# Paired Softplus, a column projection in rows of eight and a later load of the residual in a four-image scan, attention and spectral-filter kernel

## Chip, core and metric

The kernel runs on one core of a Trainium2 chip. The metric is the device time of one execution in microseconds (us). Before the change it is 5593.63 us, the median of 3 runs (5587.63 to 5597.1).

TensorE (PE, with its weight loads shown as PEld), VectorE (DVE), ScalarE (ACT), GpSimd (POOL) and SyncE (SP, which here does nothing but issue DMAs) each run a list of instructions of their own in order. They wait for one another through semaphores.

## The reference

Four images of 48 x 48 tokens and 128 channels (2304 tokens an image) pass through a state-space layer, an attention and a causal spectral filter, each with a residual:

```python
# layer 0: four scan directions k over the image after in-projection, 3x3 conv, silu
x0 = xc.reshape(B, d, L)                                  # row order
x1 = jnp.transpose(xc, (0, 1, 3, 2)).reshape(B, d, L)     # column order
xs = jnp.stack([x0, x1, x0[..., ::-1], x1[..., ::-1]], axis=1)
x_dbl = jnp.einsum('bkdl,kcd->bkcl', xs, x_proj_w)        # the x-projection
dts_r, Bs, Cs = (x_dbl[:, :, :R], x_dbl[:, :, R:R + N], x_dbl[:, :, R + N:])
dts = jnp.einsum('bkrl,kdr->bkdl', dts_r, dt_proj_w)
dt = jax.nn.softplus(dts + dt_proj_b[None, :, :, None])
...
def step(h, inp):
    dt_l, u_l, B_l, C_l = inp
    dA = jnp.exp(dt_l[..., None] * A)
    h = h * dA + (dt_l * u_l)[..., None] * B_l[:, :, None, :]
    y = jnp.einsum('bkdn,bkn->bkd', h, C_l)
    return (h, y)
...
# layer 1
t = t + _L1_attn_ref(_ln_t(t))
t = t + _L1_ffn_ref(_ln_t(t), ...)    # 16 causal FFT filters, projected and summed ("STU")
```

There are d = 256 inner channels and N = 16 states, so a direction has 4096 scans of 2304 steps.

## The kernel before

**Stages.** For each image b: a prologue (norm, in-projection, conv, silu), then the scans of the four directions, then an epilogue and the attention. The spectral filter of image b - 1 is worked out on TensorE during the scans of image b (`stu`, line 1060), interleaved by a count of matmul columns. During the scans of image 0 its place is taken by a mixture of filter weights (line 901); the filter of the last image stands alone at the end (`stu3`, line 1355). The prologue of the next image and the first part of its scans' preparation lie between the steps of the attention.

**Scans.** A direction is cut into 6 chunks of 384 columns, so an image has 24 chunks (k = 0 to 3). A chunk has 8 units (two halves h of the channels, four groups q of states), and a unit has four scans of 128 rows x 384 columns (`TENSOR_TENSOR_SCAN`, line 511). That is 192 units and 768 scans an image. For a unit, ScalarE writes the four decays exp(dt A) (line 504) and a copy of the B row (line 487) into slots of a ring in PSUM. VectorE multiplies (line 495) and scans. Three of eight units have their product on GpSimd instead, and need no copy of B. GpSimd multiplies the scanned states by C (line 521), and TensorE sums them over states (line 529). The ring has five slots for image 0 and four for the others.

**Preparation of a chunk** (`Chunk.prep`, line 380) is a generator that is advanced three times a unit, from 17 units ahead of the chunk's first (`LEAD`) over 15 units (`STEPS`). It makes, in order: the x-projection into a ring slot (line 408) and its copy to `xd` on ScalarE (line 413), for k = 0 and 1 only; the store of it (line 429; k = 2 and 3 load it again, since they run over the same columns backwards); two dt projections (line 422), each copied from a ring slot (line 425); Softplus over 128 x 768 in place (line 434), between two table loads of ScalarE, since it and exp are in different tables; the product dt x (line 452); two stores (line 441); and loads of `rep`, four DMAs for each half (line 446), that spread rows over partitions. `fetch` (line 467) brings the B and C rows, 32 DMAs a chunk (line 473).

**Order.** Schedules are written by hand: each engine's instructions stand in the order in which the Python code issues them. All DMAs that matter here are on SyncE's queue. It issues them in order, and an issue that waits holds all those behind it. Before the scans of image b + 1, `begin_scans` (line 553) advances chunk 0's preparation to its end, fetches its 32 rows, and advances those of chunks 1 and 2 a little. It is a generator too, one step for each step of the attention. The attention ends with the division of its output into `T` (lines 1013 to 1020), its store (line 1022, `td`), a load of part of it (`tu`, line 1028), a norm and transposition into `uT` (line 1053), and the store of that (`ud`, line 1055), for five pieces J of the tokens. The scans' tiles `s` take the SBUF space that `T` held.

**The spectral filter** runs over blocks of tokens and, in each, over 16 filters k. `begin` (line 1180) loads a block's input (`ux`), weights (`mue`) and residual (`res`, from `td`). `ended` (line 1242) adds the projected result to the residual (line 1244) and stores the output.

Of the kernel before, what the change touches and what calls it, by code (L numbers as in the profile page):

```python
# [8 lines left out]
F32 = mybir.dt.float32  # L9
AF = mybir.ActivationFunctionType  # L10
ALU = mybir.AluOpType
# [4 lines left out]
P = 128  # L16
B, H, W, C = 4, 48, 48, 128
# [3 lines left out]
NH = D // P  # L21
CS = 384
# [3 lines left out]
KF = 16  # L26
# [33 lines left out]
def hybrid_kernel(ctx: ExitStack, tc: tile.TileContext, a: dict, out: bass.AP):  # L60
# [3 lines left out]
    nc = tc.nc  # L64
# [3 lines left out]
    res = ctx.enter_context(tc.tile_pool(name="res", bufs=1, space=DRAM))  # L68
# [16 lines left out]
    xw = load("xw", [P, NH, 2, P], a["x_proj_wT"].rearrange("(h p) k r -> p h k r", p=P))  # L85
# [35 lines left out]
    onerow = wp.tile([P, 1], F32, name="onerow")  # L121
# [48 lines left out]
    class Slow:  # L170


        def __init__(self, f, w):
            self.f, self.w = f, w
# [153 lines left out]
    def in_order(t, k, lo, n):  # L328

        if k % 2 == 0:  # L330
            return t[:, lo // W:(lo + n) // W, :]
        return t.rearrange("p h w -> p w h")[:, lo // H:(lo + n) // H, :]
# [33 lines left out]
    class Chunk:  # L366


        def __init__(self, b, k, c):
            self.b, self.k, self.lo = b, k, c * CS  # L370
            self.name = f"{b}_{k}_{c}"
            self.bc, self.rep = {}, []
            self.rev = k >= 2
            self.first = c == (NCH - 1 if self.rev else 0)
            self.last = c == (0 if self.rev else NCH - 1)

            self.slot = CS if self.rev else 0
            self.at = slice(0, CS) if self.rev else slice(1, CS + 1)

        def prep(self, pool):  # L380

            k, name, xc = self.k, self.name, xcs[self.b]
            xdd_ = xdd[k % 2][self.lo // CS]

            def rest(n=1):

                yield
                yield 0
                yield
                for i in range(3 * n - 3):
                    yield 0 if i % 3 == 1 else None

            if k >= 2:
                xd = self.xd = pool.xd.tile([P, CS], F32, tag="xd", name=f"xd{name}")
                nc.sync.dma_start(xd, xdd_)
            yield from rest(2)  # L400
            if k < 2:
                hold = mm_hold()
            yield
            if k < 2:
                xd = self.xd = pool.xd.tile([P, CS], F32, tag="xd", name=f"xd{name}")
                ps = mm_tile(f"xp{name}", hold)
                for h in range(NH):
                    nc.tensor.matmul(ps[:, :CS], xw[:, h, k, :], in_order(xc[h], k, self.lo, CS),
                                     start=(h == 0), stop=(h == NH - 1))
            yield 2 * CS if k < 2 else 0  # L410
            yield
            if k < 2:
                nc.scalar.activation(xd, ps[:, :CS], AF.Identity, bias=onerow)
                mm_done(hold)
            yield from rest()

            re = pool.one.tile([P, NH, 2, CS], F32, tag="re", name=f"re{name}")
            for h in range(NH):
                hold = mm_hold()
                yield  # L420
                ps = mm_tile(f"dt{name}_{h}", hold)
                nc.tensor.matmul(ps[:, :CS], dtw[:, k, h * P:(h + 1) * P], xd, start=True, stop=True)
                yield CS
                yield
                nc.scalar.copy(re[:, h, 0], ps[:, :CS])
                mm_done(hold)
                if h == 0:
                    if k < 2:
                        nc.sync.dma_start(xdd_, xd)
                    yield from rest()  # L430
            yield
            yield 0

            nc.scalar.activation(re[:, :, 0], re[:, :, 0], AF.Softplus)
            yield
            yield
            yield 0
            d = dram.tile([NH, G4, DL, 2, CS], F32, tag="dtdu", name=f"dtdud{name}")

            def store(h):  # L440
                nc.sync.dma_start(d[h].rearrange("g j i t -> (g j) i t"), re[:, h])

            def load(h):
                rep = pool.rep.tile([P, G4, 2, CS], F32, tag="rep", name=f"rep{name}_{h}")
                for c in range(C4):
                    nc.sync.dma_start(rep[c::C4], d[h].rearrange("g j i t -> j g i t"))
                self.rep.append(rep)

            for h in range(NH):
                x = in_order(xc[h], k, self.lo, CS)  # L450
                dt, dx = [re[:, h, i].rearrange("p (r w) -> p r w", w=x.shape[2]) for i in range(2)]
                nc.vector.tensor_tensor(dx, dt, x, ALU.mult)
            yield
            yield
            store(0)
            yield 0
            store(1)
            yield
            yield from rest(2)
            load(0)  # L460
            yield from rest(2)
            yield
            yield 0
            load(1)
            yield
# [78 lines left out]
    POOLED = ((0, 3), (1, 1), (1, 3))  # L544
    order = [(k, c) for k in range(K) for c in (range(NCH) if k < 2 else reversed(range(NCH)))]
    quads = [(h, q) for h in range(NH) for q in range(Q4)]
    STEPS = 15
    LEAD = 17
    FETCHED = range(2 * Q4)

    CHUNK_COLS = len(quads) * CS + 3 * CS

    def begin_scans(b, pool):

        chunks = [Chunk(b, k, c) for k, c in order]
        preps = [ch.prep(pool) for ch in chunks]
        for i in range(7):
            next(preps[0])
        for i in range(3 * STEPS - 7):
            if next(preps[0]) is not None:  # L560
                yield
        for i in FETCHED:
            chunks[0].fetch(i, pool)
        for i in range(3 * (LEAD - len(quads))):
            if next(preps[1]) is not None:
                yield
        for i in range(3 * (LEAD - 2 * len(quads))):
            next(preps[2])
        yield chunks, preps

    def scans(b, chunks, preps, front, sp, back, ring, finish, work, work_cols):
# [39 lines left out]
        def prepare(s):  # L611

            ci, j = divmod(s, len(quads))
            for c in range(ci + 1, ci + 4):
                if c < len(chunks) and 0 <= s - len(quads) * c + LEAD < STEPS:
                    done[0] += next(preps[c]) or 0

        def refill(s, i):
# [46 lines left out]
            next(finish, None)  # L665
        for u in pending:
            u.add_y()
        assert next(work, None) is None

# [388 lines left out]
    def stu(b, env, seeds):  # L1060
# [15 lines left out]
        items = [(blk, k) for blk in BLOCKS for k in range(KF)]  # L1076
        tts, Gs, U, now, nxt = {}, {}, {}, {}, [0]
# [21 lines left out]
        order = [(n, cs) for n in range(len(items)) for cs in slots(n)]  # L1099
# [80 lines left out]
        def begin(n):  # L1180
            (lo, hi, place, extra), k = items[n]
            m = 2 if extra else 1

            now["x"] = pool.one.tile([P, 6, P], F32, tag="ux", name=f"ux{b}_{n}")
            nc.sync.dma_start(now["x"][:, 2:, :hi - lo], ud[:, :, 1 + lo:1 + hi])
            nc.sync.dma_start(now["x"][:, :2, :hi - lo], ud[:, 2:, lo:hi])
            now["mu"] = pool.one.tile([P, 2, 3, C], F32, tag="mue", name=f"mue{b}_{n}")
            nc.sync.dma_start(now["mu"][:, :m], mud[:, place:place + m])
            now["T", n] = pool.two.tile([P, 4, C], F32, tag="res", name=f"res{b}_{n}")
            nc.sync.dma_start(now["T", n][:hi - lo], td[4 * lo:4 * hi].rearrange("(p j) c -> p j c", j=4))  # L1190

        def parts(w, extra):
# [57 lines left out]
        tabs, ps, pool = env  # L1250
        prime()
        for n, (_, k) in enumerate(items):
            if k == 0:
                begin(n)
            yield from conv(n, 0)
            if n > 0:
                fetch_G(n - 1)
            if n > 1:
                if k == 2:
                    yield from ar(n - 2)  # L1260
                yield from project(n - 2)
            for c in (2, 1):
                yield from conv(n, c)
            if n > 1 and k == 1:
                do_late()
                yield from end(n - 2)
        n = len(items) - 1
# [236 lines left out]
    SB = bass.MemoryType.SB  # L1504
# [38 lines left out]
    run(prologue(0, turn.one, mm_tile), 3, weights(once.one))  # L1543
    turn.close()
    once.close()
    front = Stage(tc, "f0", "left", one=(1, SB), xd=(3, SB), rep=(3, SB))
    first = begun(begin_scans(0, front))
    begin0.close()
    start_y(0)
    for b in range(B):  # L1550
        sp = Stage(tc, f"h{b}", "left", s=(6, SB))
        ps = Stage(tc, f"b{b}", "right", psa=(1, PSUM), psy=(1, PSUM), psc=(1, PSUM), psp=(1, PSUM))
# [34 lines left out]
        if more:  # L1587
            env = [tabs]
            work = stu_alone(b, env)
# [17 lines left out]
                parts.pop(0)()  # L1607
        if more:
            turn.close()
            front = Stage(tc, f"f{b + 1}", "left", one=(1, SB), xd=(3, SB), rep=(3, SB))  # L1610
            start_y(b + 1)
            pieces = begin_scans(b + 1, front)
        first = None
# [81 lines left out]
```

## Time and profile before

| | |
|---|---|
| median of 3 runs | 5593.63 us (5587.63 to 5597.1) |
| profiled execution, its own time | 5603.98 us |
| its span, first to last instruction | 5602.2 us |
| mean granted TensorE clock | 0.930 |
| scans of images 0, 1, 2, 3, first to last (us in the span) | 120 to 1072, 1320 to 2322, 2566 to 3566, 3807 to 4805 |
| busy share of the span | PE 86%, DVE 78%, POOL 65%, ACT 59%, PEld 55% |
| table loads before Softplus, before exp | 95 and 89, 1283 ns each |

The whole span, in 40 slices of 140 us, with the busy share of each engine in tenths:

```profile
PE   3566556698999998898999999898999999889999
DVE  6999999856899999756999999657999999513211
ACT  2777777546777776456777776457777776432111
POOL 1899999714889998505888998406889998301100
```

VectorE is full during the four stages of scans (slices 2 to 8, 10 to 17, 19 to 26, 28 to 35). Between them lie the ends of the attention, and after the last the spectral filter of image 3, on TensorE alone. In the tables that follow, a group's line gives its count, its busy time, the mean of one in ns, and the idle time of its engine just before it with what ended most of it. A timeline's line gives the start, the duration, the instructions, and in brackets how long the engine had idled and what released it.

### The profile page before, as it was taken

Reading aid. Unit: us, or ns where it says so; the run is one execution under the profiler, and the core shown is the slowest. Engines: PE = TensorE matmul, PEld = TensorE weight load, DVE = VectorE, ACT = ScalarE, POOL = GpSimd, SP = SyncE. Lnnn points to the kernel's source line nnn. Section 1 sums busy time; section 2 is a strip of 40 time slices with the busy share of each in tenths; the row PEclk is TensorE's granted clock in tenths of the full one; section 3 lists DMA queues with packets and bytes.
Section 4 is the critical chain, followed back from the end, with each engine's and each line's share of the span. In section 5 each row is a group of like instructions: output and inputs, shape, how many; then the busy total and the mean of one; then the engine's idle time right before and its main releaser. Section 6 shows DMA issues by size and latency. Waiting matters only on the chain. (4 is left out here: it accounts for less than half of the span.)

```text
span 5602.2 us, 74057 instructions
## 1 busy us (share of the span) xinstructions
PE 4812.5 (86%) x23582; PEld 3078.9 (55%) x23582; DVE 4347.5 (78%) x5307; ACT 3324.9 (59%) x6923; POOL 3665.0 (65%) x1882
## 2 busy tenths in 40 slices
PE   3566556698999998898999999898999999889999
PEld 1211112345556666645666667645556667659987
DVE  6999999856899999756999999657999999513211
ACT  2777777546777776456777776457777776432111
POOL 1899999714889998505888998406889998301100
PEclk6877777799999999999999999999999999999999
DMA  3545545306887778516887778416878778226543
GB/s 104 164 151 169 169 158 166 116 30 174 237 241 249 254 253 264 167 33 195 234 250 245 250 253 278 132 59 196 247 241 254 254 251 279 73 64 155 143 146 94
DMA packets 741421, 1035.16 MB, mean 185 GB/s; under 512 B 142760, under 2 KB 564904, under 8 KB 740968
## 3 DMA queue, kind: packets, MB, share of 16 engines
q1 hardware_dynamic: 735208, 1027.13, 59.6%
q10 hardware_dynamic: 5824, 3.30, 0.3%
q8 instruction: 189, 3.10, 0.2%
q14 instruction: 200, 1.64, 0.1%
HBM read 911.77 MB, written 118.31 MB: 184 GB/s over the span
## 5 line engine op out<-in xcount | busy, mean ns | idle before, releaser
L511 DVE TENSOR_TENSOR_SCAN s<-ring,s 128x385 f32<-128x385 f32 x3072 | 2700.3, 937 | 127.2 <-ACT ring L504 125.9
L521 POOL TENSOR_TENSOR s<-s,bc 128x1536 f32<-128x1536 f32 x764 | 2429.0, 3182 | 128.2 <-DVE s L511 70.3
L504 ACT ACTIVATE ring<-rep,A 128x384 f32<-128x384 f32 x3072 | 1758.5, 584 | 795.6 <-DVE s L495 463.1
L495 POOL TENSOR_TENSOR s<-rep,bc 128x1536 f32<-128x1536 f32 x288 | 994.6, 3453 | 192.7 <-DMA bc<-xdd 155.7
L495 DVE TENSOR_TENSOR s<-rep,ring 128x1536 f32<-128x1536 f32 x480 | 831.0, 1731 | 83.0 <-issue 43.4
L529 PE MATMUL y<-s,csum 128*32 128x384 f32 x6144 | 717.5, 542 | 184.6 <-POOL s L521 117.1
L1154 PE MATMUL cx<-tt,u 128*128 128x252 f32 (+7 forms) x2880 | 622.4, 357 | 92.2 <-ACT cy L1170 90.8
L1154 PE MATMUL cx<-tt,us 128*128 128x252 f32 (+7 forms) x2880 | 626.2, 357 | 62.5 <-ACT U L1178 55.3
L1154 PEld LDWEIGHTS cx<-tt,u 128*128 128x128 f32 x2880 | 481.6, 193 | 303.9 <-ACT cy L1170 130.2
L1154 PE MATMUL cy<-tt,u 128*128 128x252 f32 (+5 forms) x2880 | 608.4, 353 | 33.3 <-DMA tt<-fd 33.2
L1154 PEld LDWEIGHTS cx<-tt,us 128*128 128x128 f32 x2880 | 481.9, 193 | 244.1 <-issue 91.9
L1154 PEld LDWEIGHTS cy<-tt,u 128*128 128x128 f32 x2880 | 484.8, 193 | 167.7 <-issue 116.3
L1217 PE MATMUL pr<-U,G 128*128 128x288 f32 (+6 forms) x1536 | 449.2, 422 | 12.0 <-DMA G<-gd 11.8
L529 PEld LDWEIGHTS y<-s,csum 128*32 128x32 f32 x6144 | 127.2, 112 | 545.3 <-issue 276.5
L1474 POOL TENSOR_TENSOR t<-s,s 128x512 f32<-128x512 f32 x48 | 63.4, 1321 | 545.9 <-ACT s L1472 545.9
L934 PE MATMUL G<-M,W 128*128 128x256 f32 (+3 forms) x512 | 235.5, 577 | 190.8 <-ACT W L924 87.3
L816 ACT ACTIVATE e<-s,shift 128x512 f32<-128x512 f32 (+1 forms) x360 | 231.2, 644 | 283.1 <-PE s L814 282.8
L814 PE MATMUL s<-xnT 128*128 128x512 f32 (+1 forms) x720 | 341.0, 558 | 13.0 <-ACT xnT L774 13.0
L806 PE MATMUL o<-e,xn 128*128 128x512 f32 (+1 forms) x720 | 337.4, 552 | 2.0 <-ACT e L816 2.0
L1217 PEld LDWEIGHTS pr<-U,G 128*128 128x128 f32 x1536 | 255.3, 192 | 137.8 <-issue 82.3
L519 POOL COPY carry<-s 128x4 f32<-128x4 f32 x640 | 122.2, 191 | 294.7 <-DVE s L511 289.3
L934 PEld LDWEIGHTS G<-M,W 128*128 128x128 f32 x512 | 104.4, 236 | 322.7 <-issue 136.8
(236 smaller groups left out, 5221.3 us busy)
## 6 DMA issues: line engine op xcount, KB each, us to landing
rep<-dtdud SPq DMA_DIRECT2D x768, 384.0 KB
bc<-xdd SPq DMA_DIRECT2D x3072, 48.0 KB
tt<-fd SPq DMA_DIRECT2D x144, 577.0 KB
dtdud<-re SPq DMA_DIRECT2D x192, 384.0 KB
tt<-fd SPq DMA_DIRECT2D x144, 505.0 KB
tt<-fd SPq DMA_DIRECT2D x144, 379.0 KB
G<-gd SPq DMA_DIRECT2D x160, 256.0 KB
t<-fd SPq DMA_DIRECT2D x80, 384.0 KB
```

The lines of the kernel that those rows point to most:

```text
L495: eng.tensor_tensor(s, self.ch.rep[self.h][:, :, 1], bt.unsqueeze(1).to_broadcast([P, G4, CS]), ALU.mult)
L504: nc.scalar.activation(ring.body(self.dA[g]), ch.rep[self.h][:, g, 0], AF.Exp, scale=A[:, ch.k, self.h * G4 + g, self.q:self.q + 1])
L511: nc.vector.tensor_tensor_scan(s, ring.decays(i, ch.rev), s, 0.0, ALU.mult, ALU.add)
L519: nc.gpsimd.tensor_copy(carry[:, self.h, self.q].unsqueeze(2), self.s[:, :, end:end + 1])
L521: eng.tensor_tensor(self.s, self.s, ch.bc[Q4 + self.q].unsqueeze(1).to_broadcast([P, G4, CS]), ALU.mult)
L529: nc.tensor.matmul(ch.y[g * DL:(g + 1) * DL, :CS], csum, self.s[:, g], start=(self.q == 0), stop=(self.q == Q4 - 1))
L806: nc.tensor.matmul(po[J][:, :w], xn[:, i], e[:, :w], start=(i == 0), stop=(i == NT - 1))
L814: nc.tensor.matmul(p[:, :w], xnT[:, i * P:(i + 1) * P], xnT[:, 512 * J:512 * J + w], start=True, stop=True)
L816: nc.scalar.activation(e[:, :w], p[:, :w], AF.Exp, bias=shift)
L934: nc.tensor.matmul(p[:, :n], W[:, q if t else 0, i], M[t][:, i].unsqueeze(1).to_broadcast([P, n, C]), start=(t == 0 and i == 0), stop=(t = ...
L1154: nc.tensor.matmul(p4[:, 1:3, v - (hi - at):] if g else p4[:, 0:4:3, v - (hi - at):], x, t[:, :, hi - 1 - at + J * P:end if end >= 0 else ...
L1217: nc.tensor.matmul(o if q else o.rearrange("p f r m -> p r f m"), G, U[n][:, 4 * q:4 * q + 4, v0:v1].rearrange("p (a b) m -> p a b m", a=2 ...
```

## The change

1. *Softplus for pairs of chunks.* The preparation of an even chunk rests five units (`EARLY`) before its Softplus, and that of an odd chunk runs eight units earlier than before and rests eight units after its Softplus. So the two stand one after the other on ScalarE. The time step `dt` and the product `dx` are tiles of their own (`dt0`, `dt1` by the chunk's parity, and one `dx`), and each half is stored by two DMAs of 192 KB in place of one of 384 KB. `prepare` looks at four chunks ahead rather than three. `begin_scans` prepares chunks 0 and 1 together, and parts of chunks 2 and 3. The pool of `xd` has two buffers in place of three.
2. *Column projection.* For k = 1 the x-projection reads the image as 48 rows of eight neighbouring columns rather than column by column, and the copy out of PSUM (line 413) puts the columns in order.
3. *Residual.* `res` has one buffer, and is loaded at the last but one filter of its block. At the end of the scans, what is left of the spectral filter's generator is run rather than asserted to be empty.

```diff
     class Chunk:
 
 
-        def __init__(self, b, k, c):
+        def __init__(self, b, i, k, c):
             self.b, self.k, self.lo = b, k, c * CS
+            self.odd = i % 2
             self.name = f"{b}_{k}_{c}"
             self.bc, self.rep = {}, []
             self.rev = k >= 2
...
                 xd = self.xd = pool.xd.tile([P, CS], F32, tag="xd", name=f"xd{name}")
                 ps = mm_tile(f"xp{name}", hold)
                 for h in range(NH):
-                    nc.tensor.matmul(ps[:, :CS], xw[:, h, k, :], in_order(xc[h], k, self.lo, CS),
-                                     start=(h == 0), stop=(h == NH - 1))
+                    lo = self.lo // W
+                    x = xc[h][:, :, lo:lo + CS // H] if k else xc[h][:, lo:lo + CS // W, :]
+                    nc.tensor.matmul(ps[:, :CS], xw[:, h, k, :], x, start=(h == 0), stop=(h == NH - 1))
             yield 2 * CS if k < 2 else 0
             yield
             if k < 2:
-                nc.scalar.activation(xd, ps[:, :CS], AF.Identity, bias=onerow)
+                p = ps[:, :CS]
+                if k:
+                    p = p.rearrange("p (r w) -> p w r", r=H)
+                nc.scalar.activation(xd.rearrange("p (r w) -> p r w", r=CS // W), p.rearrange("p (r w) -> p r w", w=W)
+                                     if not k else p, AF.Identity, bias=onerow)
                 mm_done(hold)
             yield from rest()
 
-            re = pool.one.tile([P, NH, 2, CS], F32, tag="re", name=f"re{name}")
+            dt = pool.one.tile([P, NH, CS], F32, tag=f"dt{self.odd}", name=f"dt{name}")
             for h in range(NH):
                 hold = mm_hold()
                 yield
...
                 nc.tensor.matmul(ps[:, :CS], dtw[:, k, h * P:(h + 1) * P], xd, start=True, stop=True)
                 yield CS
                 yield
-                nc.scalar.copy(re[:, h, 0], ps[:, :CS])
+                nc.scalar.copy(dt[:, h], ps[:, :CS])
                 mm_done(hold)
                 if h == 0:
                     if k < 2:
...
             yield
             yield 0
 
-            nc.scalar.activation(re[:, :, 0], re[:, :, 0], AF.Softplus)
+            if not self.odd:
+                yield from rest(EARLY)
+            nc.scalar.activation(dt, dt, AF.Softplus)
+            if self.odd:
+                yield from rest(len(quads))
             yield
             yield
             yield 0
+            dx = pool.one.tile([P, NH, CS], F32, tag="dx", name=f"dx{name}")
             d = dram.tile([NH, G4, DL, 2, CS], F32, tag="dtdu", name=f"dtdud{name}")
 
             def store(h):
-                nc.sync.dma_start(d[h].rearrange("g j i t -> (g j) i t"), re[:, h])
+                for i, x in enumerate((dt, dx)):
+                    nc.sync.dma_start(d[h].rearrange("g j i t -> (g j) i t")[:, i], x[:, h])
 
             def load(h):
                 rep = pool.rep.tile([P, G4, 2, CS], F32, tag="rep", name=f"rep{name}_{h}")
...
 
             for h in range(NH):
                 x = in_order(xc[h], k, self.lo, CS)
-                dt, dx = [re[:, h, i].rearrange("p (r w) -> p r w", w=x.shape[2]) for i in range(2)]
-                nc.vector.tensor_tensor(dx, dt, x, ALU.mult)
+                v, o = [y[:, h].rearrange("p (r w) -> p r w", w=x.shape[2]) for y in (dt, dx)]
+                nc.vector.tensor_tensor(o, v, x, ALU.mult)
             yield
             yield
             store(0)
...
     POOLED = ((0, 3), (1, 1), (1, 3))
     order = [(k, c) for k in range(K) for c in (range(NCH) if k < 2 else reversed(range(NCH)))]
     quads = [(h, q) for h in range(NH) for q in range(Q4)]
-    STEPS = 15
-    LEAD = 17
+    EARLY = 5
+    STEPS = (15 + EARLY, 15 + len(quads))
+    LEAD = (17 + EARLY, 17 + len(quads))
     FETCHED = range(2 * Q4)
 
     CHUNK_COLS = len(quads) * CS + 3 * CS
 
     def begin_scans(b, pool):
 
-        chunks = [Chunk(b, k, c) for k, c in order]
+        chunks = [Chunk(b, i, k, c) for i, (k, c) in enumerate(order)]
         preps = [ch.prep(pool) for ch in chunks]
-        for i in range(7):
-            next(preps[0])
-        for i in range(3 * STEPS - 7):
-            if next(preps[0]) is not None:
+        calls = [0] * len(preps)
+
+        def go(c, n):
+            for i in range(calls[c], n):
+                next(preps[c])
+            calls[c] = n
+
+        DT = 23
+        for i in range(8, DT + 4):
+            go(0, min(i, DT))
+            go(1, i - 3)
+            if i % 3 != 0:
+                yield
+        go(0, DT + 3 * EARLY)
+        go(0, DT + 3 * EARLY + 1)
+        go(1, DT + 1)
+        ends = [3 * (LEAD[c % 2] - len(quads) * c) for c in range(4)]
+        ends[0] = 3 * STEPS[0]
+        yield
+        for i in range(DT + 3 * EARLY + 2, ends[0] + 1):
+            go(0, i)
+            go(2, min(i - DT - 3 * EARLY, ends[2]))
+            if i % 3 == 0:
                 yield
         for i in FETCHED:
             chunks[0].fetch(i, pool)
-        for i in range(3 * (LEAD - len(quads))):
-            if next(preps[1]) is not None:
-                yield
-        for i in range(3 * (LEAD - 2 * len(quads))):
-            next(preps[2])
+        for c in range(1, 4):
+            go(c, ends[c])
         yield chunks, preps
 
     def scans(b, chunks, preps, front, sp, back, ring, finish, work, work_cols):
...
         def prepare(s):
 
             ci, j = divmod(s, len(quads))
-            for c in range(ci + 1, ci + 4):
-                if c < len(chunks) and 0 <= s - len(quads) * c + LEAD < STEPS:
+            for c in range(ci + 1, ci + 5):
+                if c < len(chunks) and 0 <= s - len(quads) * c + LEAD[c % 2] < STEPS[c % 2]:
                     done[0] += next(preps[c]) or 0
 
         def refill(s, i):
...
             next(finish, None)
         for u in pending:
             u.add_y()
-        assert next(work, None) is None
+        for _ in work:
+            pass
 
 
 
...
             nc.sync.dma_start(now["x"][:, :2, :hi - lo], ud[:, 2:, lo:hi])
             now["mu"] = pool.one.tile([P, 2, 3, C], F32, tag="mue", name=f"mue{b}_{n}")
             nc.sync.dma_start(now["mu"][:, :m], mud[:, place:place + m])
-            now["T", n] = pool.two.tile([P, 4, C], F32, tag="res", name=f"res{b}_{n}")
+
+        def residual(n):
+            (lo, hi, place, extra), k = items[n]
+            now["T", n] = pool.one.tile([P, 4, C], F32, tag="res", name=f"res{b}_{n}")
             nc.sync.dma_start(now["T", n][:hi - lo], td[4 * lo:4 * hi].rearrange("(p j) c -> p j c", j=4))
 
         def parts(w, extra):
...
         for n, (_, k) in enumerate(items):
             if k == 0:
                 begin(n)
+            if k == KF - 2:
+                residual(n - k)
             yield from conv(n, 0)
             if n > 0:
                 fetch_G(n - 1)
...
     run(prologue(0, turn.one, mm_tile), 3, weights(once.one))
     turn.close()
     once.close()
-    front = Stage(tc, "f0", "left", one=(1, SB), xd=(3, SB), rep=(3, SB))
+    front = Stage(tc, "f0", "left", one=(1, SB), xd=(2, SB), rep=(3, SB))
     first = begun(begin_scans(0, front))
     begin0.close()
     start_y(0)
...
                 parts.pop(0)()
         if more:
             turn.close()
-            front = Stage(tc, f"f{b + 1}", "left", one=(1, SB), xd=(3, SB), rep=(3, SB))
+            front = Stage(tc, f"f{b + 1}", "left", one=(1, SB), xd=(2, SB), rep=(3, SB))
             start_y(b + 1)
             pieces = begin_scans(b + 1, front)
         first = None
```

## The prediction

> **What bounds the kernel now.** I read the page first, then four windows from the first to the last scan of each image, then the waits of VectorE in one of them, then the timelines around a Softplus and around two starts of scans.
>
> From the page, and the table of the four windows (us; then busy us and count for PE, PEld, DVE, ACT, POOL; then clock, DMA share, GB/s):
>
> ```profile
> span 5602.2 us, 74057 instructions
> L511 DVE TENSOR_TENSOR_SCAN s<-ring,s 128x385 f32<-128x385 f32 x3072 | 2700.3, 937 | 127.2 <-ACT ring L504 125.9
> 120.00:1072.00 952.00, 562.94 (x2250) 184.72 (x2252) 911.04 (x932) 671.05 (x1403) 870.13 (x423) 0.75 0.51 160
> 2566.00:3566.00 1000.00, 930.09 (x5116) 630.76 (x5120) 929.28 (x994) 709.23 (x1526) 873.43 (x425) 0.97 0.78 244
> ```
>
> Some 3950 of the 5602 us are these four stages, and VectorE is busy 93 to 96% of each: its chain of scans sets their length. What can be won inside is VectorE's idle time, some 41 us in image 0 and 70 in each of the others. Most of it waits for a decay (line 504, exp on ScalarE):
>
> ```profile
> DVE s L511 <- ACT ring L504: 36.5, 36, 2.6
> DVE ya L541 <- PE y L529: 16.5, 9, 7.5
> DVE s L495 <- issue: 12.6, 16, 2.0
> ```
>
> One Softplus, ScalarE and then VectorE (start, duration):
>
> ```profile
> 2647.97 1.28 ACT L434 ACT_TABLE_LOAD   x1
> 2649.26 0.84 ACT L434 ACTIVATE re<-re 128x768 f32<-128x768 f32 x1
> 2650.12 1.28 ACT L504 ACT_TABLE_LOAD   x1
> ...
> 2652.03 1.94 DVE L511 TENSOR_TENSOR_SCAN s<-ring,s 128x385 f32<-128x385 f32 x2 [2.32 <-ACT ring L504]
> ```
>
> The block is 3.41 us on ScalarE (1.28 + 0.84 + 1.28 and the gaps), but VectorE stands only 2.32 of them, because decays already in the ring cover the rest. Summed over the 22 blocks of an image that lie between its scans, such stalls are 8.7 us in image 0 (five ring slots) and 26.6, 27.0, 27.4 in images 1 to 3 (four slots).
>
> The start of image 1's scans, on SyncE's queue, ScalarE and VectorE:
>
> ```profile
> 1288.86 2.53 SPq L446 DMA_DIRECT2D rep<-dtdud  x4
> 1291.49 21.24 SPq L473 DMA_DIRECT2D bc<-xdd  x32
> ...
> 1313.45 0.56 SPq L1055 DMA_DIRECT2D ud<-uT  x1
> 1314.50 0.38 SPq L1022 DMA_DIRECT2D td<-T  x1
> 1301.26 0.58 ACT L1053 COPY uT<-utr 128x512 f32<-128x512 f32 x1
> 1318.48 1.75 DVE L495 TENSOR_TENSOR s<-rep,ring 128x1536 f32<-128x1536 f32 x1 [1.64 <-DMA td<-T]
> 1320.16 2.65 DVE L511 TENSOR_TENSOR_SCAN s<-ring,s 128x385 f32<-128x385 f32 x3
> ```
>
> The second input product of the scans writes a tile whose memory belonged to the attention's T, so it waits until T is stored. That store is last in the queue; T itself is finished at 1314.47, so SyncE is hardly late: the 32 row fetches end at 1312.73, just before. Image 2 shows the same wait (1.83 us); in image 3 the last wait was 0.71 for a decay.
>
> **What the Trainium skill says.** "ScalarE: Activation LUTs", What ACT_TABLE_LOAD costs: a load is about 1283 ns, plus a drain of about 1380 for each switch of set. The trace agrees on the load (95 at line 434 and 89 at 504, all 1283 ns) and shows no drain; I use the trace. "DMA: Bandwidth & Descriptors", Anatomy of one DMA: about 2.0 us fixed, mostly the completion. The trace agrees in kind: stores issued at 1276.88, their readers at 1279.27; T's store holds its reader 3.98 us (1314.50 to 1318.48). "SBUF — State Buffer", SBUF: two separate sides: reads that leave a 16-byte line at each element pay. The trace agrees: a matmul of 384 columns in column order takes 822 ns, in row order 485.
>
> **The change, part by part.**
>
> 1. *Pairs of Softplus.* Twelve pairs of chunks an image; a pair has two loads in place of four, and its block is 1.28 + 2 x 0.84 + 1.28 = 4.25 us where two of 3.41 stood. The pair stands where the even chunk's Softplus stood. Even blocks cost VectorE 13.1 to 13.7 us an image in images 1 to 3 (of some 27); each pair is 0.84 longer, so at most 11 x 0.84 = 9.2 more: 22.5. Gain 4.5 an image, 13.5 in three. In image 0 even blocks cost 4.9, and 9.2 more less slack gives 8.7 + 2: a loss of 2. Sum about -12; bounds -30 (the longer block is covered whole: 13.5 an image from the odd blocks, less image 0) and 0 (a second row of decays runs out).
>
> 2. *Stores.* Time step and product have tiles of their own, so a chunk's 2 stores of 384 KB become 4 of 192 KB: 192 more DMAs in the kernel, 48 an image, about 0.5 us each on SyncE (0.79 for 2 at line 441 to 0.56 for one), 25 us an image. SyncE issues about 1277 DMAs for 730 us of a 1000 us stage and waits for about 210 more, partly for engines. It holds, with less slack. Also, the two chunks' holds on ring slots move: before, preparation took a slot in units 1, 3, 5 of eight, beside a unit that GpSimd enters and that needs no spread slot; after, the even chunk takes it in units 4, 6, 0, beside spreads. In units 0 to 80 of image 2, VectorE's idle was 2.7, 0.2 and 2.8 us in phases 1, 3 and 5, where holds sat, and 5.7 and 4.7 in phases 4 and 6, which get them. Together +8, bounds -9 (a hold leaves a phase that idles) and +36 (9 an image: SyncE's extra 25 not a third hidden, or one slot short all along).
>
> 3. *Column projection.* 48 matmuls (24 column chunks, two each) at a pitch of 0.645 become about 0.32 to 0.33 each: some 1.28 us of TensorE a chunk, 31 us in all. TensorE waits at its place for ring slots and isn't what the scans wait for, so I take 0 for it, except at the ends, below. ScalarE's copy at line 413 then reads PSUM with a step of eight elements; no row shows this. It is 0.57 us now; the nearest row, a strided write at line 539, went from 472 to 808 ns. Bounds 0 and 0.34 x 24 = 8; taken 0 to 2, inside the +8.
>
> 4. *End of an image's scans.* Chunks are prepared further ahead, so the count that paces the spectral work holds about 1152 columns fewer from preparation, and that work runs some 1.9 us ahead; the wait at line 541 (7.93 us at one place in image 1) and the 2.3 at line 1244 shrink by about 2 an image: -6, bounds -9 and 0.
>
> 5. *Residual.* One buffer in place of two, loaded a block's length later. In the order of VectorE the addition stands only one to one and a half scans earlier than before; it isn't behind the last scan. 0.
>
> 6. *Starts, images 1 to 3.* Chunks 0 and 1 are now prepared together ahead of the scans. The order on SyncE becomes: row stores, T's and u's transfers, four stores, 4 + 4 loads of rep, then `ud<-uT` for piece 2, then the 32 row fetches, then T's last store. Before, `ud<-uT` stood behind the fetches. SyncE issues in order, so the fetches now wait for the copy of uT on ScalarE: 1301.26 + 0.58 in this trace, where they started at 1291.49. The pair's Softplus and two more matmuls ahead of it on TensorE move the copy to between 1301 and 1304. From 1303: fetches 1303.6 to 1325, T's store 1325.5, landing 3.98 later 1329.5, product 1.75: first scan at 1331 in place of 1320.2. Behind the waiting `ud<-uT` stand exactly these: fetches, T, ux, mue. Taken +10 each, +30; bounds +4 (the fetches are issued faster than 0.66 us each, since fewer DMAs are ahead of them) and +13.
>
> 7. *Start, image 0.* Weights M come from SyncE after the row stores, now behind those of chunk 1 too. Before: M issued at 131.91, TensorE idle 33.60 for it to 135.58, projection 140.40, ScalarE blocked 12.04 to 142.33, VectorE stalled 10.35 to 143.42. After: M some 4 us later, but fewer matmuls stand between M and what ScalarE waits for: VectorE resumes about 1 later, having done 6 scans rather than 11 ahead of the stall (5 x 0.93 = 4.65). +5.5, bounds 3 and 8. Chunk 0's early stalls ease by 3.
>
> Sum: 30 + 5.5 - 3 - 12 - 6 + 8 = +22.5 on the profiled execution, whose own time is 5603.98 (span 5602.2). The runs' median is 5593.63, 10 below it; the same +22.5 gives 5616.
>
> **Rivals.**
> - *A, late starts decide (forecast):* +12 to +45; 5616.
> - *B, the pairing decides, faster.* For it: ScalarE's waits are the largest cause of idle in VectorE. If the longer block is covered, -30; starts then have to be absorbed, to +4 each; -30 - 6 + 12 + 5.5 = -18: about 5575. It decides from a start delay under 3 us each with over 20 us less of waits at line 504. Against: at 2647.97 the ring covers only 1.1 of 3.41.
> - *C, both cancel:* starts +6 each, pairing -20: 18 + 5.5 - 20 - 6 + 3 = 0; 5594.
> - *D, SyncE or the ring saturates:* the +36 bound on top, 5644. For it: DMA share 0.78 and SyncE near full. Against: rep and bc land well ahead in the waits above; neither is among VectorE's largest.
> - *The change isn't what its words say:* the residual is not moved behind the last scan; it would cost or give under 2 us, within C.
>
> **How the numbers follow.** A 0.62, D 0.12, C 0.18, B 0.08. This kernel's runs tell 0.2% (11 us) from no change. Slower 0.74, same 0.18, faster 0.08. The range takes A and D nearly whole and half of C: 5592 to 5640.
>
> **What would show it.** Table loads near 97. First scans of images 1 to 3 about 10 us later after the last attention work, with bc fetches beginning right behind `ud<-uT`; idle before line 511 for line 504 near 110. L408's columns near 485 ns. I'm wrong if the fetches keep starting 22 us ahead of T's end, or if waits at line 504 fall below 95.

## The result, and the profile after

The changed kernel takes 5635.03 us (median of 4 runs, 5628.28 to 5643.96) where the kernel before takes 5590.63 (4 runs): a ratio of 1.0076, 95% interval 1.0063 to 1.009. It is slower by some 43 us. The forecast was 5616 (22.5 us slower), its range 5592 to 5640.

Two lines of the page:

```profile
span 5642.2 us, 74282 instructions
L523 DVE TENSOR_TENSOR_SCAN s<-ring,s 128x385 f32<-128x385 f32 x3072 | 2697.5, 940 | 148.1 <-ACT ring L516 147.9
```

The page's span is 40.0 us longer than before. VectorE's idle time ahead of a scan, nearly all for decays, which the pairs were to shorten, has grown from 127.2 to 148.1 us. Read by stages (first to last scan of each image, from the timelines of VectorE), the 40 us lie here:

| us | before | after | difference |
|---|---|---|---|
| start of image 0's scans | 120.1 | 123.2 | +3.1 |
| scans of image 0 | 951.4 | 950.4 | -1.0 |
| last scan of an image to first of the next, 0 to 1, 1 to 2, 2 to 3 | 248.6, 244.1, 241.8 | 257.4, 254.4, 254.2 | +31.5 |
| scans of images 1, 2, 3 | 1002.0, 999.6, 997.0 | 1001.8, 1001.5, 1001.4 | +6.1 |
| last scan to the end | 797.6 | 798.1 | +0.5 |

The table compares two single executions, and before's (5603.98 us) was itself 13 us above its median, the changed kernel's (5643.96) 9 above. The scans of images 1 to 3 together took 2998.6 us before and 2986.7 in a kernel whose time can't be told from it (the residual's part alone, below). So this table can't tell the +6.1 from no change; what the scans lost is measured by the experiments.

Three quarters of the loss in the table are the starts of images 1 to 3. The start of image 1's scans, on SyncE, ScalarE and VectorE:

```profile
1298.52 2.77 SPq L458 DMA_DIRECT2D rep<-dtdud  x4
1305.29 0.54 SPq L1085 DMA_DIRECT2D ud<-uT  x1
1305.94 20.31 SPq L485 DMA_DIRECT2D bc<-xdd  x32
1326.35 0.52 SPq L1052 DMA_DIRECT2D td<-T  x1
...
1304.68 0.58 ACT L1083 COPY uT<-utr 128x512 f32<-128x512 f32 x1
1329.25 1.75 DVE L507 TENSOR_TENSOR s<-rep,ring 128x1536 f32<-128x1536 f32 x1 [12.28 <-DMA td<-T]
1330.92 3.50 DVE L523 TENSOR_TENSOR_SCAN s<-ring,s 128x385 f32<-128x385 f32 x4
```

T itself is done at 1314.60, hardly later than the 1314.47 of before. But its store is issued 11.75 us after that, behind 32 row fetches, and VectorE stands 12.28 us for it. From the end of T to the first scan it takes 16.3, 16.4 and 16.0 us; before it took 5.7, 5.9 and 4.8.

A pair of Softplus in image 2, on ScalarE and VectorE:

```profile
2625.54 1.28 ACT L442 ACT_TABLE_LOAD   x1
2626.84 1.58 ACT L442 ACTIVATE dt<-dt 128x768 f32<-128x768 f32 x2
...
2628.52 1.28 ACT L516 ACT_TABLE_LOAD   x1
2630.50 2.66 DVE L523 TENSOR_TENSOR_SCAN s<-ring,s 128x385 f32<-128x385 f32 x3 [3.62 <-ACT ring L516]
```

The pair does what it says: 48 loads stand at line 442 and 45 at 516, where 95 and 89 stood, and the stalls near the blocks are 23.2, 24.1 and 24.0 us in images 1 to 3 (26.6, 27.0, 27.4 before). The growth to 148.1 us comes from elsewhere. TensorE's waits for tables and weights of the spectral filter, over the whole span (us, times, longest), before and after:

```profile
PE cx L1154 <- DMA tt<-fd: 5.7, 4, 2.4
PE pr L1217 <- DMA G<-gd: 11.8, 6, 4.1
PE cy L1154 <- DMA tt<-fd: 33.2, 14, 6.2
```

```profile
PE cx L1184 <- DMA tt<-fd: 37.9, 23, 3.4
...
PE pr L1250 <- DMA G<-gd: 24.3, 12, 6.0
PE cy L1184 <- DMA tt<-fd: 20.1, 22, 2.0
```

Together they grew from 50.7 to 82.3 us: TensorE waits more for SyncE's loads. ScalarE copies the filter's results in the order written, between decays, so a late result holds the decays behind it. In the scans of images 1 to 3 its waits for these results grew from 284.9 to 336.3 us, and VectorE's waits for decays from 109.2 to 127.0. VectorE's wait for y has grown too, from 52.9 to 61.9 us over the span.

### The profile page after: what moved, and what is told of

It reads as the page before. It is cut to its first block, busy times and chain, and to the rows that moved or that the text cites. A ratio compares the mean times of both kernels' runs of the same rounds, so it can differ in the third digit from the quotient of the medians.

```text
span 5642.2 us, 74282 instructions
## 1 busy us (share of the span) xinstructions
PE 4802.8 (85%) x23582; PEld 3087.5 (55%) x23582; DVE 4329.7 (77%) x5307; ACT 3209.1 (57%) x6829; POOL 3664.3 (65%) x1882
## 5 line engine op out<-in xcount | busy, mean ns | idle before, releaser
L523 DVE TENSOR_TENSOR_SCAN s<-ring,s 128x385 f32<-128x385 f32 x3072 | 2697.5, 940 | 148.1 <-ACT ring L516 147.9
```

Of the source, the lines that this page charges most:

```text
L523: nc.vector.tensor_tensor_scan(s, ring.decays(i, ch.rev), s, 0.0, ALU.mult, ALU.add)
```

## The experiments

The kernel before was run again beside each set (medians 5589 to 5593), so the ratios are compared. One profiled execution differs from another by up to 7 us in a stage that is the same: from the last scan to the end it was 792 to 799 us in all kernels. Differences of a stage below that are not read from a profile.

### Are the starts late because of the order on SyncE's queue?

First the order alone: the last step of the preparation is joined to the one before, which puts the fetches ahead of `ud<-uT` again.

```diff
-            if i % 3 == 0:
+            if i % 3 == 0 and i < ends[0]:
                 yield
         for i in FETCHED:
             chunks[0].fetch(i, pool)
```

> The changed kernel, with the 32 row fetches of chunk 0 put back ahead of the store ud<-uT of piece 2, as they stood before. Theory (lateness has two parts: ud<-uT in front of the fetches, and the pair's Softplus that makes the rep loads in front of them late): the fetches begin right behind rep's second loads, near 1301.4 in place of 1305.9, so the first scans of images 1 to 3 come some 4.5 us earlier each: 13 us less than the changed kernel, about 5622, ratio to before 1.0055. Rival 1 (the place of ud<-uT alone makes the lateness): 30 less, about 5605. Rival 2 (the loss is inside the scans): no change, 5635.

5624.34 us, ratio 1.0067 (1.0053 to 1.0081), which overlaps the interval of the changed kernel. The start of image 2's scans, on SyncE and VectorE:

```profile
2550.94 22.91 SPq L485 DMA_DIRECT2D bc<-xdd  x32
2573.95 0.56 SPq L1085 DMA_DIRECT2D ud<-uT  x1
2574.61 0.57 SPq L1052 DMA_DIRECT2D td<-T  x1
...
2578.66 1.75 DVE L507 TENSOR_TENSOR s<-rep,ring 128x1536 f32<-128x1536 f32 x1 [11.99 <-DMA td<-T]
```

From T's end to the first scan it still takes 16.2, 16.0 and 15.7 us. In image 1 the fetches start at 1301.84, 4.1 us earlier than in the changed kernel, right behind rep, as in the kernel before. But they take longer (22.5 us for 20.3; 22.9 in the lines above), `ud<-uT` is issued after them, and the product follows T's store after 4.35 us (4.05 in the lines above) rather than 2.90, so the 4 us are lost again. The median is near the theory's 5622, but the 4.5 us a start from which that was worked out aren't there, and rival 1 falls: the place of `ud<-uT` alone isn't what costs. What the traces leave is that rep's loads end 10 us later than before (1301.3 against 1291.4 in image 1). Chunk 0's Softplus now stands beside chunk 1's: it starts at 1291.64, before at 1275.12. That this is why rep is late is read from the order of the traces; no run takes it away alone.

So the fetches were taken apart instead. The four B rows go ahead of chunk 0's stores, where SyncE idles; each C row goes into the scans, shortly before its first use.

```diff
         ends[0] = 3 * STEPS[0]
         yield
+        for i in FETCHED[:Q4]:
+            chunks[0].fetch(i, pool)
...
-        for i in FETCHED:
-            chunks[0].fetch(i, pool)
...
             real = s < len(units)
+            for i in ((0, 1), (2,), (3,))[s] if s < 3 else ():
+                chunks[0].fetch(Q4 + i, front)
             enter(s)
```

> The changed kernel, with chunk 0's four B rows fetched ahead of its stores and its four C rows in the scans, just before they are needed. Theory (the start of the scans waits for SyncE's queue): T's last store is issued as soon as T is done, so the first scans of images 1 to 3 come some 10 us earlier each, as before the change; in image 0 the weights M are issued some 10 us earlier, and the 10.63 us stall of VectorE nearly goes: about 40 us less than the changed kernel, 5595, ratio 1.0008. Rival (the fetches were hidden, or the late C rows hold up GpSimd): under 15 us less, 5620 or more.

5576.34 us, ratio 0.9975 (0.9966 to 0.9985): 56 us less than the changed kernel by the ratios, and faster than before. Image 1's start, on SyncE and VectorE:

```profile
1275.53 10.05 SPq L485 DMA_DIRECT2D bc<-xdd  x16
...
1304.47 0.38 SPq L1054 DMA_DIRECT2D td<-T  x1
1304.90 4.96 SPq L485 DMA_DIRECT2D bc<-xdd  x8
...
1308.56 3.50 DVE L523 TENSOR_TENSOR_SCAN s<-ring,s 128x385 f32<-128x385 f32 x4
```

T is done at 1304.44, and its store follows at once. To the first scan it is 4.1, 4.2 and 4.1 us, 36 us less in three starts. In image 0 the weights M are issued at 124.45 rather than 134.42, and VectorE's stall falls from 10.63 to 1.51 us. The theory gave 40; profile against profile the starts and that stall give 45. The other 11 are not placed: the scans of image 1 are 8 us shorter, little more than executions differ by.

The same late C rows in the kernel before, with nothing of the change:

> The kernel before, with chunk 0's four C rows fetched in the scans, nothing of the change. Theory: image 0's stall for the weights M (10.35 us) goes for the most part, and from T's end to the first scan it takes some 4.2 us in place of 4.8 to 5.9: together 8 to 13 us less than before, about 5580. If instead this reaches the time of the changed kernel with both repairs (5546), then the pairs of Softplus bring nothing.

5583.45 us, 0.9988 (0.9982 to 0.9994): some 7 us less, just under the 8 to 13 expected. From T's end to the first scan it takes 4.1, 4.2 and 4.1 us, as stated, but the stall for M falls only by half, to 5.03 us. The repair is worth some 7 us there and 56 in the changed kernel (1.0076 to 0.9975), so most of its gain, some 50, undoes a loss of the change. (In the kernel before only the C rows were moved, in the changed one the B rows too.)

### The stores, and the loss inside the scans

In the changed kernel, one store takes both halves of dt and one both halves of dx:

```diff
-                for i, x in enumerate((dt, dx)):
-                    nc.sync.dma_start(d[h].rearrange("g j i t -> (g j) i t")[:, i], x[:, h])
+                nc.sync.dma_start(d.rearrange("h g j i t -> (g j) h i t")[:, :, h], (dt, dx)[h])
```

> The changed kernel, with a chunk's four stores of 192 KB joined to two of 384 KB (both halves of dt, both halves of dx); tiles and order of everything else as changed. Theory S (48 more DMAs an image on SyncE make the filter's tables and weights late, TensorE waits for them, and VectorE for TensorE's sums): 10 to 15 us less, about 5622; waits of TensorE for tt and G fall from some 80 us to before's some 55, and VectorE's wait for y from 57 to some 48. Rival H (the moved holds of ring slots make the loss inside the scans): within 4 us of 5635.

5604.55 us, ratio 1.0025 (1.0013 to 1.0036): 29 us less by the ratios, twice what S gave. H falls as the cause: the holds of ring slots are where they were. The scans of images 1 to 3 took 994.5, 991.1 and 984.9 us rather than some 1001.6. TensorE's waits for the same loads:

```profile
PE cx L1183 <- DMA tt<-fd: 26.1, 19, 3.3
PE pr L1249 <- DMA G<-gd: 18.3, 7, 5.9
PE cy L1183 <- DMA tt<-fd: 13.8, 13, 2.5
```

58.2 in place of 82.3 us. In the scans of images 1 to 3, ScalarE's waits for the filter's results fell from 336.3 to 285.0 us (284.9 before) and VectorE's waits for decays from 127.0 to 114.9. The wait for y over the span, 57.3, did not fall to 48. So each step of the path from SyncE to VectorE goes back, most of the way, when the stores are joined. On SyncE itself both the time spent on issuing and the waits for earlier DMAs to land fell (in image 2 from 745.6 to 733.0 us and from 124.8 to 116.9); which of the two counts stays open.

The reverse, four stores in the kernel before:

```diff
-                nc.sync.dma_start(d[h].rearrange("g j i t -> (g j) i t"), re[:, h])
+                for i in range(2):
+                    nc.sync.dma_start(d[h].rearrange("g j i t -> (g j) i t")[:, i], re[:, h, i])
```

> The kernel before, with each of its two stores a chunk cut in two of 192 KB, nothing else changed. Theory S: 10 to 15 us slower than before, about 5603, with more wait of TensorE for tt and G. Rival H: within 4 us of 5591.

5596.36 us, 1.0012 (1.0005 to 1.002): some 7 us, between the two. TensorE's waits did not grow (46.3 us), so here the path above isn't what costs. What did fall is SyncE's own wait for TensorE to free a table's buffer: 180 us before, 144 with four stores, 131 in the changed kernel with two stores and 108 with four. It tells how far ahead SyncE is, not how long the kernel takes: in the changed kernel with B and C rows taken apart, 56 us faster, it is 68 us.

So 192 further stores cost 7 us in one kernel and 29 in the other. One more run asks whether faster scans alone make that difference: four stores in the kernel before with its projection in rows of eight.

> The kernel before with the projection in rows of eight (5580) and with four stores a chunk. Theory F (SyncE is a floor: the faster the scans, the more 48 further DMAs an image cost): 15 us or more above 5580, about 5596. Rival G (the cost of four stores belongs to the paired schedule): about 5 above, 5585.

5595.4 us, 1.0004 (0.9995 to 1.0013), where the projection alone gives 0.9985 (below): 0.0019 or some 11 us, between F and G. Why the stores cost most in the paired schedule stays open.

### The other parts alone

The projection in rows of eight, put into the kernel before:

> The kernel before with the column projection in rows of eight alone. Theory (TensorE isn't what the scans wait for, and the copy that reorders costs little): within 4 us of 5591; the 48 matmuls take some 485 ns in place of 822. Rival (TensorE, busy for 93% of a stage, paces the scans by way of y): 10 us less or more.

5579.89 us, 0.9985 (0.9977 to 0.9992): some 8 us less. The interval is 4.5 to 13 us, so the theory's 4 at most lies just outside it and the rival's 10 inside. The path is not the rival's, though: in the scans of images 1 to 3 the wait for y hardly changed (48.0 to 46.1 us), while ScalarE's waits for the filter's results fell from 284.9 to 253.6 and VectorE's for decays from 109.2 to 101.3. The reordering copy costs nothing: 572 ns a copy over ten chunks of both orders, where it took 570 to 580 before.

The residual's part, put into the kernel before:

> The kernel before with the residual's later load and its single buffer alone. Theory: a DMA moves by a block's length, nothing waits for it: within 4 us of 5591. Rival (a single buffer makes the load wait for the addition and holds SyncE's queue): 5 us slower or more.

5584.08 us, 0.9992 (0.9983 to 1.0001): no difference that these runs can tell.

### Both repairs

The changed kernel with B and C rows taken apart and two stores a chunk:

> The changed kernel with both repairs: chunk 0's B rows ahead of its stores and C rows in the scans, and two stores of 384 KB a chunk. Theory (two separate losses, each on SyncE's queue: 36 us of late starts, 30 us inside the scans): the gains add up, 5576 - 30 = 5546, ratio to before 0.992; each of the stages of images 1 to 3 between 985 and 994 us. Rival (both repairs relieve the same delay): 5560 to 5576.

5559.08 us (5557.44 to 5561.6), ratio 0.9951 (0.9939 to 0.9964). This is the fastest kernel of the study, 27 us below before and 70 below the changed kernel by the ratios. Alone the repairs give 56 and 29, so 15 of their gains overlap; the time lies just below the rival's span, not at the theory's 5546. By the sums the losses are mostly separate; the theory's full addition isn't there. The stages of images 1 to 3 took 993.2, 987.3 and 993.0 us, within the 985 to 994 that the theory gave.

What is left of the change without its losses? The same kernel with the projection in column order again:

> The changed kernel with both repairs (5559), but the column projection in column order as before. What is left of the change is the pairs of Softplus and the residual. Theory P (the pairs give a gain of their own inside the scans, 4 to 5 us an image): about 5567, some 16 less than the kernel before with its C rows fetched late (5583). Rival Q (only the projection in rows of eight gains, the pairs nothing): 5580 or more.

5566.56 us, 0.9954 (0.994 to 0.9967), 0.0034 or 19 us below the kernel before with late C rows (0.9988). And the kernel before with late C rows and rows of eight, without pairs:

> The kernel before with its C rows fetched late and the projection in rows of eight, without pairs: the gains of 6 and 9 us add up, about 5574. If the pairs gain, the changed kernel with both repairs (5559) stays some 15 us below this; if they don't, the two are within 5 us.

5576.07 us, 0.9968 (0.9955 to 0.998), 0.0017 or some 10 us above the kernel with pairs; here the intervals overlap. The pairs (with the residual's part and the earlier B rows, which neither comparison separates from them) gain 10 to 19 us once nothing eats it: theory P holds by the first comparison, whose intervals are apart, and Q falls.

## Why the prediction was right, point by point

The forecast was slower, and slower it is, within the range; but 43 us is nearly twice the 22.5 of the sum. The late starts (rival A) came as worked out. On top came most of rival D (29 us for its 36), to which the prediction gave 0.12: the measured 5635 lies between A's 5616 and D's 5644, nearer D's.

- *Part 6, starts of images 1 to 3: right in size and place, half right in the cause.* Taken +30; from T's end to the first scan it became 32 us longer in all. The first scan of image 1 stands at 1330.92, where 1331 was worked out. That it agrees to 0.1 us is luck: T's store was issued at 1326.35, 0.8 later than the 1325.5 worked out, and the product followed it after 2.90 us, 1.1 sooner than the 3.98 taken. The prediction put the lateness down to the fetches' place behind `ud<-uT`. In image 1 the fetches start 14.4 us later than before; rep's loads, which end 10 us later, make most of that, and the place makes 4. The first experiment took the 4 away and nothing was won. By the traces the pair's late Softplus is behind the 10, which the prediction didn't count. Moving the fetches off T's path removed the loss.
- *Part 7, start of image 0: right in kind.* VectorE resumes from the stall having done 6 scans rather than 11, as stated, but at 142.13, 1.3 us earlier than before rather than 1 later. That makes some 3.4 us, where 5.5 were taken. M came 2.5 us later, not 4, and the stall was 10.63 for 10.35. The +2.1 of the table up to the end of image 0's scans holds this, the eased stalls and the pairs' loss in image 0 together.
- *Part 1, pairs: right in kind.* The stalls near the blocks fell by 9.7 us in images 1 to 3 (13.5 forecast) and rose by 2.5 in image 0 (2 forecast). As a gain in time it could be seen only with the losses removed: 10 to 19 us for 12.
- *Part 2, stores: the term that was mis-sized.* "It holds, with less slack ... Together +8": joining the stores again gave 29 us. It lies within the bounds kept for it (-9 to +36), and its 21 us above the +8 are about as large as the whole miss from 5616 to 5635. The reasoning that failed is rival D's "against": "rep and bc land well ahead in the waits above; neither is among VectorE's largest". That is so in the changed kernel too. In this kernel a crowded SyncE doesn't appear as a DMA wait of VectorE. It makes tables for TensorE late (50.7 to 82.3 us), which makes results late that ScalarE copies between decays (284.9 to 336.3), and appears as VectorE's wait for decays (109.2 to 127.0). The other half of the +8, the moved holds of ring slots, was not run alone.
- *Part 4, end of the scans: right there, undone elsewhere.* In the last 24 units VectorE's waits before lines 541 and 1244 fell from 48.5 to 37.6 us over three images (a fall of 6 forecast), but over the whole span the wait for y grew by 9.
- *Part 3, projection: wrong alone.* Taken at nothing, since TensorE "isn't what the scans wait for"; alone it gives some 8 us, by the traces by way of ScalarE's waits for the filter's results. Beside the pairs and repairs the ratios differ by 0.0003, less than can be told. The 1.28 us a chunk were right (2.75 to 1.45 us), but they take four matmuls of TensorE a chunk, as the trace shows, not the two of the text.
- *Part 5, residual: right*, within what can be told.

Of the signs listed, the table loads (97 in all), line 408's columns (485 ns) and the fetches right behind `ud<-uT` came as stated; the idle time before the scan for decays was to be near 110 and is 147.9.

## What to carry to other kernels

When preparation is paired or moved, write down the order on the DMA queue at the next start, with the transfer on which that start waits: anything long in front of it is paid in full. Fetch by first use; rows that are needed only after the first result don't belong ahead of it. And count the DMAs of the issuing queue: an engine that looks free of DMA waits may wait for a crowded queue by way of two other engines.

## What the runs showed that was not expected

- 32 row fetches of 48 KB took 20.3 us to issue when SyncE had idled for some 4 us ahead of them (image 1, changed), and 21.2 us (before) to 22.9 us (first experiment) right behind loads of 384 KB: 0.63 and 0.66 to 0.72 us each.
- A matmul that reads 384 columns as 48 runs of eight took 485 ns, as long as in row order; in column order it took 822.
- ScalarE's copy of 128 x 384 out of PSUM with a step of eight elements cost no more than without (576 ns a copy, for three of row chunks and for five of column chunks).
- SyncE's slack shows in its waits for a buffer to come free, hardly in its busy time: from before to after the busy time of a stage rose by 2% (729 to 746 us in image 2), and the waits fell from 180 to 108 us over the span. Neither tells the time of a kernel: with B and C rows taken apart they are 753 and 68 us, and that kernel is faster than before.
